# Scores and values of a two-layer attention kernel on 64x64 quadrants of the array, and VectorE's order around them

## The chip, the cores and the metric

The kernel runs on one core of one Trainium2 chip. The metric is the device time of one execution in microseconds (us), the median of several runs. Profiles are of one further execution. PE is TensorE (PEld its weight loads), DVE is VectorE, ACT is ScalarE, POOL is GpSimd and SP is SyncE.

## What is computed

Eight images x of 256 channels and 32 x 32 positions go through two layers; all numbers are fp32. S is 1024 positions, a head has 64 channels.

```python
# layer 0
qkv = (xt @ w_qkv + b_qkv).reshape(B, S, 8, 3 * 64)
q, k, v = split(qkv, 3, axis=-1)
attn = einsum('bihd,bjhd->bijh', q, k) * SCALE
attn = softmax(attn, axis=1)                 # over the queries i
res = einsum('bijh,bjhd->bihd', attn, v)
x = res @ w_out + b_out + xt
# layer 1
t = t + attention(layer_norm(t), W)          # one head of 256 channels
t = t + mixture_of_experts(layer_norm(t))    # 8 experts, the best 2 per token
```

In layer 0 the softmax runs over the queries, so that each key j has a maximum and a sum over all 1024 queries. The kernel therefore holds keys on the partitions and queries along the row: one row of scores has all that the softmax of a key needs, and the division by the sum can be put on the key's value vector instead of on the 1024 weights.

## The kernel before

One image after the other goes through layer 0 (`layer0`), layer 1's attention (`attend`) and the routing. The experts of the first seven images are computed together after layer 0 of the last image; the last image is done with all eight experts beside the collecting of the others' results.

`layer0` has 32 steps, (g, j): g is one of four pairs of heads, j one of eight blocks of 128 keys. A step makes the scores of both heads (`score`, L390): for head h and half n of the queries, one matmul of the head's 64 channels (partitions h * 64 and up) and 128 keys, into one bank of the score tile `psc`, which has two banks and comes from a pool of three. VectorE takes the negated maximum of the first half (`first_max`, L401) and then that of the second half together with the first (`soften`, L413). ScalarE takes the exponential of the whole tile with that maximum and sums it (L423). VectorE takes the reciprocal of both heads' sums (L430) and multiplies the step's values with it (L432, `vs`). Two steps later (LAG), `gather_values` multiplies `vs` with the exponentials and adds to `po` (L448): two banks, one for each half of the queries, head 0 on partitions 0 to 63 and head 1 on 64 to 127, accumulated over the eight blocks of keys. After the last block ScalarE copies both banks to `res` (L457), and the next pair of heads takes the same two banks.

The order on TensorE is written out in the loop at the end of `layer0`. In turn `at` it issues the first half of head 0 of this step, the second half of head 1 of the step before, the second half of head 0 and the first half of head 1 of this step, and then four matmuls of the values of step `at` - 2. In blocks 3 and 5 of the first three pairs it also projects queries or keys of the next pair (`project`, L299; VectorE takes them out of PSUM, L289). On VectorE the order is set in part by `issue_after`. From the second image on, the routing of the image before (`gates`, `dispatch`) is a generator that is taken one portion further in each turn: small VectorE operations first, then 16 portions of a cast (L764) and a scattering DMA that GpSimd issues (L766). In the last image the plan of the experts (`plan_blocks`) lies beside the last steps.

SyncE's queue holds transfers only. During layer 0 these are the load of the next image (`load_x`, L92) and the store of the sums of the image before (L1160), both issued ahead of the first values. For the first image it also fills the rows and packs the experts' weights (L245 to L277).

Of the kernel before, what the change touches and what calls it, by code (L numbers as in the profile page):

```python
# [10 lines left out]
F32 = mybir.dt.float32  # L11
I32 = mybir.dt.int32
AF = mybir.ActivationFunctionType
ALU = mybir.AluOpType
AX = mybir.AxisListType


@with_exitstack
def kernel(
# [23 lines left out]
    nc = tc.nc  # L43
    P = 128
# [3 lines left out]
    DK = 64  # L48
    SCALE = DK ** (-0.5)
    NCC = C // P  # L50
    NT = S // P
    NH2 = S // 512
# [316 lines left out]
    def layer0(b, xT, begun, routing):  # L369

        v, qks = begun.v, begun.qks
        array = None
        res = one.tile([P, NPAIR, S], F32, tag="res", name=f"res_{b}")
        steps = [(g, j) for g in range(NPAIR) for j in range(NT)]
        LAG = 2
        seconds = {}  # L380
        pss, firsts, nmaxes, exps, sums, vss = {}, {}, {}, {}, {}, {}
        po = None

        def score(at, h, n):
            g, j = steps[at]
            q, k = qks[g]
            if n == 0:
                pss[at, h] = big(f"psc_{b}_{g}_{j}_{h}")
            r = slice(h * DK, (h + 1) * DK)
            mm = nc.tensor.matmul(  # L390
                pss[at, h][:, ts(n, 512)], k[r, ts(j, P)], q[r, ts(n, 512)], start=True, stop=True
            )
            if n == 1:

                tc.declare_no_dep(mm.ins, firsts.pop((at, h)).ins, reason="the other bank")

        def first_max(at, h):

            g, j = steps[at]
            nmax = small.tile([P, 1], F32, tag="nmax1", name=f"nmax1_{b}_{g}_{j}_{h}")  # L400
            firsts[at, h] = nc.vector.tensor_reduce(  # L401
                nmax, pss[at, h][:, ts(0, 512)], AX.X, ALU.max, negate=True
            )
            nmaxes[at, h] = nmax

        def soften(at, h):

            g, j = steps[at]
            ps = pss.pop((at, h))
            if h == 0:  # L410
                sums[at] = small.tile([P, 2], F32, tag="sums", name=f"sums_{b}_{g}_{j}")
            nmax = small.tile([P, 1], F32, tag="nmax", name=f"nmax_{b}_{g}_{j}_{h}")
            seconds[h] = nc.vector.tensor_scalar(  # L413
                scrap,
                ps[:, ts(1, 512)],
                -1.0,
                nmaxes.pop((at, h)),
                ALU.mult,
                ALU.min,
                accum_out=nmax,  # L420
            )
            ex = expp.tile([P, 1024], F32, tag="exps", name=f"ex_{b}_{g}_{j}_{h}")
            nc.scalar.activation(  # L423
                ex, ps, AF.Exp, bias=nmax, scale=1.0, accum_out=sums[at][:, h : h + 1]
            )
            exps[at, h] = ex
            if h == 1:

                rs = small.tile([P, 2], F32, tag="rs", name=f"rs_{b}_{g}_{j}")
                nc.vector.reciprocal(rs, sums.pop(at))  # L430
                vs = four.tile([P, 2, DK], F32, tag="vs", name=f"vs_{b}_{g}_{j}")
                nc.vector.tensor_mul(  # L432
                    vs,
                    v[:, j, ts(g, P)].rearrange("p (h d) -> p h d", d=DK),
                    rs.unsqueeze(2).to_broadcast([P, 2, DK]),
                )
                vss[at] = vs

        def gather_values(at):
            nonlocal po  # L440
            g, j = steps[at]
            if j == 0:
                po = [acc(f"po_{b}_{g}_{n}") for n in range(NH2)]
            vs = vss.pop(at)
            exs = [exps.pop((at, h)) for h in range(2)]
            for n in range(NH2):
                for h in range(2):
                    mm = nc.tensor.matmul(  # L448
                        po[n][h * DK : (h + 1) * DK, :],
                        vs[:, h, :],  # L450
                        exs[h][:, ts(n, 512)],
                        start=(j == 0),
                        stop=(j == NT - 1),
                    )
            if j == NT - 1:
                for n in range(NH2):
                    nc.scalar.copy(res[:, g, ts(n, 512)], po[n])  # L457
            return mm

        last = len(steps) - 1  # L460
        for at in range(last + LAG + 1):
            if at <= last:
                score(at, 0, 0)
            if 0 < at <= last + 1:
                score(at - 1, 1, 1)
                soften(at - 1, 1)
            if at <= last:

                with tc.issue_after(seconds[1].ins) if 1 in seconds else nullcontext():
                    first_max(at, 0)  # L470
                score(at, 0, 1)
                score(at, 1, 0)
                soften(at, 0)
                with tc.issue_after(seconds[0].ins):
                    first_max(at, 1)
            if at == 0:
                begun.rest()
                next(routing, None)
            if at >= LAG:
                array = gather_values(at - LAG)  # L480
            if at <= last:
                g, j = steps[at]
                if g + 1 < NPAIR and j in (3, 5):
                    if j == 3:
                        qks.append([])
                    qks[g + 1].append(project(b, xT, g + 1, len(qks[g + 1])))
                if array is not None:
                    with tc.issue_after(firsts[at, 1].ins), tc.issue_after(array.ins):
                        next(routing, None)
        for _ in routing:  # L490
            pass


        t1 = one.tile([P, NT, C], F32, tag="t1", name=f"t1_{b}")
        n = 1024 // C
        for i in range(0, NT, n):
            pt = big(f"pt_x_{b}_{i}")
            for j in range(n):
                for cc in range(NCC):
                    nc.tensor.transpose(  # L500
                        pt[:, j * C + cc * P : j * C + (cc + 1) * P], xT[:, cc, ts(i + j, P)], ident
                    )
            nc.vector.tensor_add(
                t1[:, i : i + n, :],
                pt.rearrange("p (j c) -> p j c", c=C),
                b_o.unsqueeze(1).to_broadcast([P, n, C]),
            )
        for i in range(NT):
            pr = acc(f"pr_{b}_{i}")
            for g in range(NPAIR):  # L510
                nc.tensor.matmul(  # L511
                    pr[:, :C], res[:, g, ts(i, P)], wo[:, g, :], start=(g == 0), stop=(g == NPAIR - 1)
                )
            nc.vector.tensor_add(t1[:, i, :], pr[:, :C], t1[:, i, :])
        return t1
# [703 lines left out]
```

## Time and profile before

| | |
|---|---|
| median of 3 runs | 2549.14 us (2547.66 to 2549.50) |
| the profiled execution's own time | 2515.67 us |
| its span in the profile | 2513.9 us |
| mean granted clock of TensorE | 0.995 |
| TensorE busy | 2475.7 us, 98% |
| VectorE busy | 1547.4 us, 62% |
| ScalarE busy | 890.6 us, 35% |
| layer 0 of the second image: from 285.96 us to about 439 us | 153 us |

The profiled execution was shorter than the median of the runs by 33 us. A program matmul in fp32 shows as two matmul records and two weight loads. A line of the groups reads: line, engine, operation, out<-in, sizes, count, then busy time and the mean in ns of one, and the idle time ahead of it with what ended it. A line of the timeline reads: start, length, engine, line, operation, and in brackets the idle time before and what ended it.

### The profile page before, as it was taken

How to read it: one execution, taken by the hardware profiler on the slowest of the kernel's cores; microseconds unless marked ns; L12 is line 12 of the kernel's file. 1: busy time of each engine (PE TensorE's matmuls, PEld its weight loads, DVE VectorE, ACT ScalarE, POOL GpSimd, SP SyncE). 2: the span in 40 equal slices, each digit the busy share in tenths (PEclk: the TensorE clock that was granted, in tenths of full speed). 3: DMA queues.
4: the chain of work that ended last, by engine and by line, in shares of the span. 5: the costliest groups of instructions: out<-in, count | busy, mean ns of one | idle time of the engine just before them, and what ended most of it. 6: DMA issues, size and time to landing. Idle time of an engine off the chain costs nothing.

```text
span 2513.9 us, 27737 instructions
## 1 busy us (share of the span) xinstructions
PE 2475.7 (98%) x9919; PEld 1300.1 (52%) x9919; DVE 1547.4 (62%) x3836; ACT 890.6 (35%) x1491; POOL 385.7 (15%) x383
## 2 busy tenths in 40 slices
PE   9999999999999999999999999999999999999799
PEld 3346533653366335633563356434643388886476
DVE  5765677557755775577647764777467753334653
ACT  2551355124512452155314441354135512221222
POOL 0000002000200010001100010001000334444652
PEclk9999999999999999999999999999999999999899
DMA  7992000000000000000000010000000256664353
GB/s 284 385 360 69 34 3 32 17 17 0 28 24 17 1 24 28 9 9 18 34 1 17 13 38 1 17 11 24 1 17 7 74 171 220 213 212 141 125 174 115
DMA packets 82515, 187.62 MB, mean 75 GB/s; under 512 B 13992, under 2 KB 23880, under 8 KB 80584
## 3 DMA queue, kind: packets, MB, share of 16 engines
q1 hardware_dynamic: 57368, 118.65, 13.2%
q0 software_dynamic: 25008, 67.20, 8.5%
q8 instruction: 78, 1.28, 0.2%
q14 instruction: 61, 0.50, 0.1%
HBM read 100.49 MB, written 110.90 MB: 84 GB/s over the span
## 4 chain that ended last, share of the span: by engine, by line
PE 93%; DVE 3%; DMA 2%; ACT 1%; issue 1%; SPq 0%; ACTq 0%; POOL 0%; POOLq 0%; DVEq 0%
PE psc L390 20%; PE po L448 19%; PE pqk L299 9%; PE py L571 9%; PE ps L545 8%; PE pr L511 4%; PE pv L335 4%; PE ph L906 4%; PE pe L931 3%; PE pdy L1113 2%; PE px L530 2%; PE pa L564 2%; PE pdh L1089 2%; PE pt_n L232 1%; PE px L896 1%; DMA wb_x<-wpack,w_at 1%
## 5 line engine op out<-in xcount | busy, mean ns | idle before, releaser
L423 ACT ACTIVATE ex<-psc,nmax 128x1024 f32<-128x1024 f32 x512 | 570.6, 1114 | 556.8 <-DVE scrap L413 492.8
L390 PE MATMUL psc<-qk,qk 64*128 64x512 f32 x2048 | 549.4, 621 | 4.2 <-ACT ex L423 4.0
L448 PE MATMUL po<-ex,vs 128*64 128x512 f32 x2048 | 495.9, 605 | 0.0
L413 DVE TENSOR_SCALAR_CACHE_REDUCE scrap<-psc,nmax 128x512 f32<-128x512 f32 x512 | 384.2, 750 | 160.1 <-PE psc L390 128.0
L390 PEld LDWEIGHTS psc<-qk,qk 64*128 64x128 f32 x2048 | 208.6, 185 | 326.2 <-ACT ex L423 173.4
L401 DVE TENSOR_REDUCE nmax<-psc 128x1 f32<-128x512 f32 x512 | 347.2, 678 | 9.5 <-PE psc L390 9.5
L448 PEld LDWEIGHTS po<-ex,vs 128*64 128x64 f32 x2048 | 124.8, 136 | 335.4 <-issue 211.8
L766 POOL DMA_INDIRECT rows<-n,d_at x112 | 108.9, 972 | 946.5 <-DVE d_at L764 940.0
L571 PE MATMUL py<-n,aT 128*128 128x256 f32 x1024 | 239.9, 388 | 4.8 <-DVE aT L566 4.8
L545 PE MATMUL ps<-nT,xa 128*128 128x512 f32 x512 | 236.5, 592 | 0.0
L299 PE MATMUL pqk<-xT,wqkv 128*128 128x512 f32 x512 | 235.0, 602 | 0.0
L571 PEld LDWEIGHTS py<-n,aT 128*128 128x128 f32 x1024 | 192.8, 192 | 68.6 <-DVE aT L566 43.7
L556 ACT ACTIVATE ex<-ps,nmax 128x1024 f32<-128x1024 f32 x64 | 71.3, 1115 | 341.1 <-DVE nmax L553 334.4
L692 POOL TENSOR_TENSOR t<-t,n 128x2048 f32<-128x2048 f32 x8 | 36.2, 4531 | 905.7 <-issue 629.8
L576 DVE SCALAR_TENSOR_TENSOR t<-py,rs,t 128x256 f32<-128x256 f32 x64 | 31.0, 484 | 215.4 <-PE py L571 215.4
L299 PEld LDWEIGHTS pqk<-xT,wqkv 128*128 128x128 f32 x512 | 93.3, 190 | 132.5 <-issue 93.6
L289 DVE TENSOR_SCALAR qk<-pqk,b_qk 128x512 f32<-128x512 f32 x100 | 75.1, 751 | 110.3 <-PE pqk L299 110.3
L545 PEld LDWEIGHTS ps<-nT,xa 128*128 128x128 f32 x512 | 93.6, 190 | 79.9 <-issue 73.6
L978 POOL DMA_INDIRECT yk<-y,yat x112 | 112.7, 1006 | 92.8 <-DVE o L1010 43.6
L335 PE MATMUL pv<-wqkv,xT 128*128 128x512 f32 x256 | 119.6, 597 | 1.1 <-ACT wqkv L105 1.1
L553 DVE TENSOR_REDUCE nmax<-ps 128x1 f32<-128x1024 f32 x64 | 78.3, 1224 | 59.7 <-PE ps L545 59.7
L511 PE MATMUL pr<-wo,res 128*128 128x256 f32 x512 | 111.8, 379 | 0.0
(191 smaller groups left out, 2439.2 us busy)
## 6 DMA issues: line engine op xcount, KB each, us to landing
rows<-wb SPq DMA_DIRECT2D x7, 8192.0 KB, 51.3
y<-yb SPq DMA_DIRECT2D x63, 256.0 KB, 2.7
xT<-in_x_dram SPq DMA_DIRECT2D x7, 1024.0 KB, 4.9
sums<-t SPq DMA_DIRECT2D x7, 1024.0 KB, 4.4
o<-sums SPq DMA_DIRECT2D x7, 1024.0 KB, 7.7
out_dram<-oT SPq DMA_DIRECT2D x14, 512.0 KB, 5.8
wpack<-in_L_ffn_w_dram SPq DMA_DIRECT2D x4, 1024.0 KB
wb<-in_L_ffn_w_dram SPq DMA_DIRECT2D x16, 256.0 KB, 2.9
```

The lines of the kernel that those rows point to most:

```text
L299: mm = nc.tensor.matmul(pq[:, ts(n, 512)], wqkv[:, cc, t, ts(g, P)], xT[:, cc, ts(n, 512)], start=(cc == 0), stop=(cc == NCC - 1),)
L335: nc.tensor.matmul(pv, self.xT[:, cc, ts(i, P)], wqkv[:, cc, 2, :], start=(cc == 0), stop=(cc == NCC - 1),)
L390: mm = nc.tensor.matmul(pss[at, h][:, ts(n, 512)], k[r, ts(j, P)], q[r, ts(n, 512)], start=True, stop=True)
L401: firsts[at, h] = nc.vector.tensor_reduce(nmax, pss[at, h][:, ts(0, 512)], AX.X, ALU.max, negate=True)
L413: seconds[h] = nc.vector.tensor_scalar(scrap, ps[:, ts(1, 512)], -1.0, nmaxes.pop((at, h)), ALU.mult, ALU.min, accum_out=nmax,)
L423: nc.scalar.activation(ex, ps, AF.Exp, bias=nmax, scale=1.0, accum_out=sums[at][:, h : h + 1])
L448: mm = nc.tensor.matmul(po[n][h * DK : (h + 1) * DK, :], vs[:, h, :], exs[h][:, ts(n, 512)], start=(j == 0), stop=(j == NT - 1),)
L511: nc.tensor.matmul(pr[:, :C], res[:, g, ts(i, P)], wo[:, g, :], start=(g == 0), stop=(g == NPAIR - 1))
L545: nc.tensor.matmul(psc[:, ts(n, 512)], xa[:, ec, ts(i, P)], nT[:, ec, ts(n, 512)], start=(ec == 0), stop=(ec == NCC - 1),)
L571: nc.tensor.matmul(py[:, :D], aT[:, ts(m, P)], n1[:, m, :], start=(m == 0), stop=(m == NT - 1))
L766: nc.gpsimd.indirect_dma_start(out=view[:, :], out_offset=bass.IndirectOffsetOnAxis(ap=at, axis=0), in_=n2[:, i, :], in_offset=None,)
L978: nc.gpsimd.indirect_dma_start(out=yk[:, i, k, :], out_offset=None, in_=self.group.y[:, :], in_offset=bass.IndirectOffsetOnAxis(ap=ats[k][ ...
```

## The change

Scores: each matmul of 64 channels by 128 keys becomes two of 64 by 64, one for each half of the keys, which go to partitions 0 to 63 and 64 to 127 of the same bank.

Values: each matmul of 128 keys by 64 channels becomes two of 64 keys. They are issued in two turns. In a turn, keys 0 to 63 go to one bank of `po` and keys 64 to 127 to the other; in the second turn the banks change places. So each bank is added to by the lower and the upper keys one after the other. Between two turns that add to the same bank, an ordering is put in with an empty instruction (`relay.nop()`) that waits for the one turn's matmul and that the next turn's first matmul waits for. It is issued on GpSimd for the first image and on SyncE for the others. The first turn stands between the two pairs of score matmuls, the second after them.

VectorE: the reciprocal and `vs` move into a function `divide`. They stood, by `issue_after`, around the first maximum of the next step's head 1: the reciprocal ahead of it, `vs` behind. Now both stand behind the second maximum of the next step's head 0 and ahead of the first maximum of its head 1.

The number of instructions on VectorE and ScalarE stays as it is. The two copies out of `po` (L457) keep their place on ScalarE, behind the exponential of the same turn's head 0, with the second bank first.

```diff
+BEHIND = mybir.DependencyInfo(mybir.DependencyClass.Sync, mybir.DependencyReason.DATA)
...
-        seconds = {}
+        seconds, turned = {}, {}
+
+        relay = nc.gpsimd if b == 0 else nc.sync
...
-            mm = nc.tensor.matmul(
-                pss[at, h][:, ts(n, 512)], k[r, ts(j, P)], q[r, ts(n, 512)], start=True, stop=True
-            )
-            if n == 1:
-
-                tc.declare_no_dep(mm.ins, firsts.pop((at, h)).ins, reason="the other bank")
+            for c in range(2):
+                mm = nc.tensor.matmul(
+                    pss[at, h][ts(c, DK), ts(n, 512)],
+                    k[r, j * P + c * DK : j * P + (c + 1) * DK],
+                    q[r, ts(n, 512)],
+                    start=True,
+                    stop=True,
+                )
+                if n == 1:
+
+                    tc.declare_no_dep(mm.ins, firsts[at, h].ins, reason="the other bank")
...
+        def divide(at):
+
+            g, j = steps[at]
+            rs = small.tile([P, 2], F32, tag="rs", name=f"rs_{b}_{g}_{j}")
+            nc.vector.reciprocal(rs, sums.pop(at))
+            vs = four.tile([P, 2, DK], F32, tag="vs", name=f"vs_{b}_{g}_{j}")
+            divided = nc.vector.tensor_mul(
...
+        def gather_values(at, turn):
...
+            past = dict(turned)
+            for half in range(2):
+                keys = ts(half, DK)
+                n = (half + turn) % 2
                 for h in range(2):
                     mm = nc.tensor.matmul(
-                        po[n][h * DK : (h + 1) * DK, :],
-                        vs[:, h, :],
-                        exs[h][:, ts(n, 512)],
-                        start=(j == 0),
-                        stop=(j == NT - 1),
+                        po[n][ts(h, DK), :],
+                        vss[at][keys, h, :],
+                        exps[at, h][keys, ts(n, 512)],
+                        start=(j == 0 and turn == 0),
+                        stop=(j == NT - 1 and turn == 1),
                     )
+                    if h == 0 and (j > 0 or turn > 0):
+                        tc.add_manual_dep(mm.ins, past[1 - half].ins.name, BEHIND)
+
+                turned[half] = relay.nop()
+                tc.add_manual_dep(turned[half].ins, mm.ins.name, BEHIND)
...
                 score(at - 1, 1, 1)
                 soften(at - 1, 1)
+            if at >= LAG:
+                gather_values(at - LAG, 0)
...
                 with tc.issue_after(seconds[0].ins):
+                    ahead = divide(at - 1) if at > 0 else seconds[0]
+                with tc.issue_after(ahead.ins):
                     first_max(at, 1)
+            elif at == last + 1:
+                divide(last)
...
             if at >= LAG:
-                array = gather_values(at - LAG)
+                array = gather_values(at - LAG, 1)
```

More of the change, by code (lines that the diff above doesn't have):

```diff
@@ L426, in soften @@
             exps[at, h] = ex
[L427 to L437, printed above, removed]
@@ L439, in gather_values @@
-        def gather_values(at):
+        def divide(at):
[4 more added lines that the diff above has]
+            divided = nc.vector.tensor_mul(
+                vs,
+                v[:, j, ts(g, P)].rearrange("p (h d) -> p h d", d=DK),
+                rs.unsqueeze(2).to_broadcast([P, 2, DK]),
+            )
+            vss[at] = vs
+            return divided
@@ L440, in gather_values @@
+        def gather_values(at, turn):
             nonlocal po
             g, j = steps[at]
-            if j == 0:
+            if j == 0 and turn == 0:
                 po = [acc(f"po_{b}_{g}_{n}") for n in range(NH2)]
-            vs = vss.pop(at)
-            exs = [exps.pop((at, h)) for h in range(2)]
-            for n in range(NH2):
+            past = dict(turned)
+            for half in range(2):
+                keys = ts(half, DK)
+                n = (half + turn) % 2
                 for h in range(2):
@@ L455, in gather_values @@
+                        stop=(j == NT - 1 and turn == 1),
+                    )
+                    if h == 0 and (j > 0 or turn > 0):
+                        tc.add_manual_dep(mm.ins, past[1 - half].ins.name, BEHIND)
+                turned[half] = relay.nop()
+                tc.add_manual_dep(turned[half].ins, mm.ins.name, BEHIND)
+            if turn == 0:
+                return mm
+            vss.pop(at)
+            for h in range(2):
+                exps.pop((at, h))
             if j == NT - 1:
```

## The prediction

> **What bounds the kernel now.** I read the page first: TensorE is busy for 98% of the span and holds 93% of the chain that ended last; layer 0's scores (L390) and values (L448) have 39% of that chain between them. No other engine is near.
>
> ```profile
> PE 2475.7 (98%) x9919; PEld 1300.1 (52%) x9919; DVE 1547.4 (62%) x3836; ACT 890.6 (35%) x1491; POOL 385.7 (15%) x383
> ...
> L390 PE MATMUL psc<-qk,qk 64*128 64x512 f32 x2048 | 549.4, 621 | 4.2 <-ACT ex L423 4.0
> L448 PE MATMUL po<-ex,vs 128*64 128x512 f32 x2048 | 495.9, 605 | 0.0
> ```
>
> The shape before the operand says which part of the array an instruction uses: scores 64 rows x 128 columns, values 128 x 64. Each program matmul is two records (1024 in the program, 2048 here). Next the timeline, for what a record costs where nothing is switched, and for what runs side by side.
>
> ```profile
> 276.25 3.60 PE L299 MATMUL pqk<-xT,wqkv 128*128 128x512 f32 x8
> ...
> 279.69 1.88 PE L335 MATMUL pv<-wqkv,xT 128*128 128x512 f32 x4
> ...
> 284.96 1.07 PE L599 MATMUL pl<-n2T,rT 128*32 128x256 f32 x16
> ```
>
> Eight whole-array records take 279.69 - 276.25 = 3.44 us, 0.43 each: I call this a slot. The 16 records of pl (256 columns, four column strips) fill 1.07 us where one after the other would be 16 x 0.215 = 3.44, so four strips do run together. Then one step of layer 0:
>
> ```profile
> 402.69 2.04 PE L390 MATMUL psc<-qk,qk 64*128 64x512 f32 x8
> ...
> 403.87 0.75 DVE L413 TENSOR_SCALAR_CACHE_REDUCE scrap<-psc,nmax 128x512 f32<-128x512 f32 x1 [0.69 <-PE psc L390]
> ...
> 404.55 0.68 DVE L401 TENSOR_REDUCE nmax<-psc 128x1 f32<-128x512 f32 x1
> ...
> 404.66 1.94 PE L448 MATMUL po<-ex,vs 128*64 128x512 f32 x8
> ...
> 405.35 0.75 DVE L413 TENSOR_SCALAR_CACHE_REDUCE scrap<-psc,nmax 128x512 f32<-128x512 f32 x1
> ...
> 406.03 0.16 DVE L430 RECIPROCAL rs<-sums 128x2 f32<-128x2 f32 x1
> 406.11 0.67 DVE L401 TENSOR_REDUCE nmax<-psc 128x1 f32<-128x512 f32 x1
> 406.20 1.11 ACT L423 ACTIVATE ex<-psc,nmax 128x1024 f32<-128x1024 f32 x1 [0.27 <-DVE rs L430]
> ...
> 406.53 2.06 PE L390 MATMUL psc<-qk,qk 64*128 64x512 f32 x8
> 406.69 0.28 DVE L432 TENSOR_TENSOR vs<-v,rs 128x128 f32<-128x128 f32 x1
> 406.89 0.15 DVE L764 CAST d_at<-d_to 128x1 int32<-128x1 f32 x1
> ```
>
> Scores start at 402.69, values at 404.66, scores again at 406.53: a step is 3.84 (3.87 in the next). Its 16 records run in pairs, so 8 slots = 3.43. The other 0.41 is two changes between 64x128 and 128x64, 0.20 each. VectorE is free for about 0.67 a step, waiting for scores. Last, where one pair of heads ends (8 steps):
>
> ```profile
> 410.04 1.11 ACT L423 ACTIVATE ex<-psc,nmax 128x1024 f32<-128x1024 f32 x1 [0.28 <-DVE rs L430]
> ...
> 411.14 1.07 ACT L457 COPY res<-po 128x512 f32<-128x512 f32 x2
> ...
> 412.35 0.20 PEld L448 LDWEIGHTS po<-ex,vs 128*64 128x64 f32 x4 [0.76 <-ACT res L457]
> ```
>
> ScalarE copies the sums out of po behind an exponential, and the next values need them gone. Scores cover this just now: 410.38 to 412.35 is the usual 1.97.
>
> **What the skill says.** TensorEngine Tiling (Array Packing), Key Properties: a change of tiling mode, not of the tile, drains TensorE, and tiles work independently; the 0.20 per change agrees. Same page, Gotcha 1: different row tiles may not use one PSUM bank at the same time; that is why the change needs its relay, and the trace shows no such case. TensorE: Matmul & The Clock Gate, Measured speedup vs the span model: row and column tiles compose (16 tiles gave 10.6x). Pairs by row and strips by column are in this trace, quadrants are not.
>
> **The change, part by part.** Times are in us; a step begins with its first set of scores at 0.
>
> *Quadrants.* Scores and values become 2048 + 2048 instructions of 64x64, four at a time: a set is two slots, 0.86, and a step is scores, values, scores, values = 8 slots = 3.43, with no change of mode. Less is excluded, since each record still streams 512 columns; more is rival 3 or the 3.60 below. The 24 plain steps per image can save 0.41. The six with a projection (128x128) had three changes and keep two: 0.20 each. Issue is no limit by pl: 32 loads and matmuls went out in its 1.07, 0.033 each, where a slot of four quadrants has 0.43/8 = 0.054.
>
> *The relay.* A value set waits for the empty instruction on SyncE (GpSimd in image 0) that waits for the set before. Behind it on TensorE stand all later matmuls. Its cover is one score set: the earlier set's last record starts at 0.43 and is modelled at 0.59, so it ends at 1.02, and the next value set is due at 1.72: 0.70. No row has this trip. Bounds from hops: TensorE to VectorE 0.05, VectorE to GpSimd 0.27 (403.19 to 403.46), ScalarE to a weight load 0.15; so 0.2 to 0.5. I take 0.35: hidden, nothing. Were the scores gone (the image's last two steps), it costs about 0.5. On SyncE the queue ahead holds the image's load and the sums store, issued at 285.65 and 286.09, long before the first values at 297.54; GpSimd is empty in image 0 until its addition at 281.09.
>
> *VectorE's order.* vs now runs ahead of the second head's first maximum and needs the reciprocal. Start to start: second maximum 0.68, first maximum to the second that uses it 0.80, second maximum 0.68, reciprocal to vs 0.20 (0.16 and 0.04 for the dependence), vs 0.20, first maximum 0.80: 3.36, under 3.43. But the loop through everything is tight: third set at 1.72, VectorE 1.07 later (402.69 to 403.87, less 0.11 of mode change) at 2.79, then 0.68 + 0.20 + 0.20 + 0.80 to the next second maximum at 4.67, exponential 0.85 later (405.35 to 406.20), 1.11 long, 0.20 to the matmul (0.15 to its load, as above, and 0.05): 6.83, where the scores that take this buffer are due at 6.86. I take 3.46 per plain step; bounds 3.43 (all hidden) and 3.60 (reciprocal and vs as late as 0.14 more). Saving 24 x 0.39 + 6 x 0.20 = 10.6 per image, x8 = **-84.5**.
>
> *Head-pair ends.* The second maximum at 2.79 leads to the exponential at 3.64, the copies 1.10 later, 1.07 long, and 0.14 to TensorE: 5.95. The next values are now due after one score set only, at 3.43 + 0.86 = 4.29. Stall 1.66, three times per image: 24 x 1.66 = **+40**. Bounds 0 and 2.0 each.
>
> *Routing work.* For images 1 to 7 the previous image's routing runs on VectorE between a first and a second maximum. About 0.22 of it (one small operation or a cast) hides in the 0.80. Before, the idle 0.67 took the rest; now it is on the tight loop. Three operations add 0.5, four add 0.75. In steps beside a projection they hide (it gives 3.4). Left are steps 6, 7, 8 (0.5 each) and 14, 16 (0.75 each): 3.0, less 0.3 of slack: 2.7 x 7 = **+19**. Bounds 0 and 30. The plan for the experts puts some 7 on VectorE in image 7's last steps; about **+4** more than now is exposed.
>
> *Ends of an image.* The first values fit into a wait for exponentials (-0.4), the last two steps wait for the relay (+0.6): **+1** in all.
>
> **Sum.** -84.5 + 40 + 19 + 4 + 1 = -20. The profiled span is 2513.9, its own time 2515.7: 2495. The median of the runs is 2549.1, 33 above that execution, and I carry the difference over: **2529**.
>
> **Rivals.**
> 1. TensorE alone decides (0.25): exponentials, copies and routing find cover, as they do now, and 84 is gained: 2465; with half of the stalls, 2495. For it: nothing but TensorE waits today. Against: the copies' chain has no slack even now.
> 2. The relay is late (0.18), the case that ends slower. Place: each of 60 value sets per image, 480 in all. It decides from 0.70, and 20/480 = 0.04 beyond eats the gain. At 0.85: 480 x 0.15 = +72: 2601. For it: three engines' queues lie in it, and no row shows the way back from SyncE. Against: each hop that is seen is at most 0.27.
> 3. Quadrants don't run four wide, so that the change doesn't do what it says (0.05): a set takes four slots, a step 6.9; far above 3000. Against: rows and columns each overlap here.
>
> **How the numbers follow.** My case has 0.52, with a range of its own from 2505 to 2550. The range that should hold 8 in 10 is 2466 to 2580: it leaves out rival 3, over half of rival 2 and a little of rival 1, and takes in plain steps of 3.60 (27 more) and the stalls' upper bounds in part. A measurement tells about 0.2% (5 us) from no change. Faster: 0.25 + 0.44 of mine = 0.69. Same: 0.06. Slower: 0.17 of rival 2, 0.05 and 0.03 = 0.25.
>
> **What would show it.** Right: rows with 64*64 at 4096 records each, score and value sets 0.86 apart, plain steps near 3.45, TensorE's wait for the copies up from 18 us to some 55, VectorE's idle for scores nearly gone. Value loads that wait for SyncE in plain steps would be rival 2; sets of 1.7 rival 3; head-pair ends without a stall, or routing steps as short as plain ones, rival 1.

## The result, and the profile after

| | before | after |
|---|---|---|
| median of 4 runs each | 2549.32 us | 2526.41 us (2521.92 to 2530.92) |
| ratio, with its 95% interval | | 0.9908 (0.9883 to 0.9932) |
| the profiled execution's own time | 2515.67 us | 2521.92 us |
| layer 0, sum over the eight images | 1225.2 us | 1197.2 us |
| from layer 0's end to the next layer 0 | 107.51 us | 108.05 us |
| from layer 0's end in the last image to the program's end | 509.4 us | 539.4 us |

The change made the kernel faster by 22.9 us; 20 had been forecast. The two profiled executions can't be set against each other as wholes. What follows layer 0 of the last image, which the change does not touch, depends on the job, that is, on which runs were made together. It took 531 to 540 us in every profile of a later job in which the kernel before ran at 2544 us, and 509 to 512 in every profile of three jobs in which it ran at 2516 to 2518, old and new kernels alike. Of the two profiles here, the one of before has the short stage and the one of after the long one. So I compare stages. "Layer 0" is from an image's first score record to the start of its last value record. There the change gains 27.9 us, and 7 x 0.54 = 3.8 are given back behind it: 24.1, which agrees with the medians.

First the page of the changed kernel: busy time by engine, then the rows of the scores and the values.

```profile
PE 2421.3 (96%) x14015; PEld 1334.8 (53%) x14015; DVE 1565.1 (62%) x3836; ACT 887.7 (35%) x1491; POOL 386.4 (15%) x383
...
L463 PE MATMUL po<-ex,vs 64*64 64x512 f32 x4096 | 612.8, 593 | 25.4 <-ACT res L482 21.3
L395 PE MATMUL psc<-qk,qk 64*64 64x512 f32 x4096 | 613.4, 596 | 17.3 <-ACT ex L432 16.3
```

There are twice as many records, of 64x64, and each is about as long as one of 64x128 was (596 ns against 621). The busy times of these two rows don't tell how wide they run, since the rows overlap; the timeline below does: a set of eight records is followed by the next set after 0.86. That is two slots of 0.43, so four records run at a time. (Eight of 64x128 held TensorE for 1.97, 402.69 to 404.66 in the timeline of before: four slots and a change of mode.) New is the idle time ahead of the values: 21.3 us that ended with ScalarE's copies. It had been 0.0 on that row.

Next the timeline of the changed kernel, image 0: the last plain step of a pair of heads, and the pair's end.

```profile
67.63 1.04 PE L395 MATMUL psc<-qk,qk 64*64 64x512 f32 x8
...
68.49 1.04 PE L463 MATMUL po<-ex,vs 64*64 64x512 f32 x8
...
69.35 1.04 PE L395 MATMUL psc<-qk,qk 64*64 64x512 f32 x8
...
69.78 0.15 PEld L463 LDWEIGHTS po<-ex,vs 64*64 64x64 f32 x4 [0.28 <-POOLq L473]
70.20 1.04 PE L463 MATMUL po<-ex,vs 64*64 64x512 f32 x8
...
71.06 1.04 PE L395 MATMUL psc<-qk,qk 64*64 64x512 f32 x8
...
71.27 1.11 ACT L432 ACTIVATE ex<-psc,nmax 128x1024 f32<-128x1024 f32 x1 [0.34 <-DVE rs L441]
...
72.38 1.06 ACT L482 COPY res<-po 128x512 f32<-128x512 f32 x2
...
73.01 0.20 PEld L463 LDWEIGHTS po<-ex,vs 64*64 64x64 f32 x4 [1.79 <-ACT res L482]
73.01 1.13 PE L463 MATMUL po<-ex,vs 64*64 64x512 f32 x6 [0.91 <-ACT res L482]
...
73.49 0.14 PEld L463 LDWEIGHTS po<-ex,vs 64*64 64x64 f32 x2 [0.29 <-ACT res L482]
...
73.92 0.60 PE L395 MATMUL psc<-qk,qk 64*64 64x512 f32 x2
...
73.97 0.59 PE L463 MATMUL po<-ex,vs 64*64 64x512 f32 x2
```

A set starts every 0.86, and a step is 71.06 - 67.63 = 3.43. The value load at 69.78 waited for the empty instruction (here on GpSimd), but 0.42 ahead of its matmul at 70.20, which is on time. At the pair's end the values were due at 71.92; the copies, which stand behind the exponential of 71.27, let the first half go at 73.01 and the second at 73.49. From then on score and value records stand between one another in groups of two. I read this as the upper and the lower 64 rows of the array, the two row groups, running out of phase until the next projection brings them together; the trace doesn't name a record's rows.

The lengths of all steps say the same at a glance (worked out from the trace; a step is sixteen score records, counted from the image's first):

```
after, image 0   5.98 2.74 3.85 7.27 3.43 7.23 3.43 3.43 3.43 3.43 4.63 7.64 3.43 7.23 3.43 3.43 3.43 3.43 4.63 7.64 3.43 7.23 3.43 3.43 3.43 3.43 4.63 3.67 3.43 3.43 3.43
after, image 3   6.19 2.80 3.85 7.27 3.43 7.23 3.43 3.84 3.80 3.95 4.59 8.09 3.73 7.42 3.43 4.09 3.43 4.09 4.59 7.64 3.43 7.23 3.43 3.43 3.43 3.43 4.63 3.67 3.43 3.43 3.44
after, image 1   6.19 2.80 3.83 7.72 8.84 7.69 3.43 3.84 3.80 3.95 4.59 8.09 3.73 7.49 3.43 4.09 3.43 4.09 4.59 7.64 3.43 7.23 3.43 3.43 3.43 3.43 4.63 3.67 3.43 3.43 3.43
```

A step with a projection is 7.23, and a pair's end costs 4.63 - 3.43 = 1.20 and 7.64 - 7.23 = 0.41 in the next step: 1.61. (Behind the third end, which no projection follows, the second part is 0.24 in the next step, and the rest at the image's end.) Image 3 has the routing of the image before on VectorE: single steps of 3.8 to 4.1. Image 1 has one thing more, near its first projection (7.72, 8.84 and 7.69 for 7.27, 3.43 and 7.23). In the timeline of that place:

```profile
299.97 2.42 PE L395 MATMUL psc<-qk,qk 64*64 64x512 f32 x8
...
302.29 2.66 PE L463 MATMUL po<-ex,vs 64*64 64x512 f32 x14
...
303.81 1.11 ACT L432 ACTIVATE ex<-psc,nmax 128x1024 f32<-128x1024 f32 x1 [7.53 <-PE po L463]
...
305.59 2.63 PE L463 MATMUL po<-ex,vs 64*64 64x512 f32 x13
```

Fourteen and thirteen value records in a row: the program's order on TensorE is another one here. All values of two steps stand bunched behind the projection, and ScalarE is without work for 7.53 us.

Layer 0 by image, for the kernels of this study (us):

| kernel | image 0 | image 1 | images 2 to 6, usual | image 7 | sum |
|---|---|---|---|---|---|
| before | 151.7 | 152.7 | 152.75 | 156.2 | 1225.2 |
| after | 145.0 | 154.9 | 148.6 | 154.2 | 1197.2 |
| no_copies | 140.2 | 150.4 | 144.0 | 148.3 | 1159.3 |
| old_tiles_no_copies | 151.9 | 152.7 | 152.7 | 156.2 | 1225.2 |
| old_tiles_new_order | 151.7 | 152.9 | 152.9 | 156.0 | 1226.1 |
| quadrants_old_order | 160.8 | 171.6 | 164.7 | 168.5 | 1325.3 |
| quadrants_old_pinned | 148.8 | 156.2 | 150.5 | 154.5 | 1212.2 |
| relay_pool_1 | 145.0 | 154.3 | 148.6 | 154.4 | 1196.8 |
| relay_pool_all | 145.0 | 154.3 | 154.2 | 163.9 | 1234.3 |
| routing_split | 145.0 | 147.9 | 147.4 | 151.6 | 1181.4 |
| split_late | 143.6 | 146.5 | 146.0 | 151.6 | 1171.4 |
| split_project | 141.8 | 144.7 | 144.65 | 150.3 | 1160.0 |
| split_copies_first | 142.5 | 144.7 | 144.5 | 148.7 | 1158.3 |
| all_mended | 141.0 | 143.8 | 143.8 | 148.0 | 1151.7 |

### The profile page after: what moved, and what is told of

It reads as the page before. It is cut to its first block, busy times and chain, and to the rows that moved or that the text cites. A ratio compares the mean times of both kernels' runs of the same rounds, so it can differ in the third digit from the quotient of the medians.

```text
span 2520.2 us, 37152 instructions
## 1 busy us (share of the span) xinstructions
PE 2421.3 (96%) x14015; PEld 1334.8 (53%) x14015; DVE 1565.1 (62%) x3836; ACT 887.7 (35%) x1491; POOL 386.4 (15%) x383
## 4 chain that ended last, share of the span: by engine, by line
PE 72%; DVE 9%; ACT 3%; issue 2%; DMA 1%; another core or an unknown queue 1%; ACTq 0%; DVEq 0%; SPq 0%; POOLq 0%
PE po L463 13%; PE psc L395 12%; PE pqk L300 8%; PE py L602 7%; PE ps L576 6%; PE pr L542 4%; PE ph L937 4%; PE pe L962 3%; PE pv L336 3%; DVE scrap L422 3%; PE pdy L1144 2%; PE pdh L1120 2%; PE px L561 2%; PE pa L595 2%; ACT ex L432 2%
## 5 line engine op out<-in xcount | busy, mean ns | idle before, releaser
L463 PE MATMUL po<-ex,vs 64*64 64x512 f32 x4096 | 612.8, 593 | 25.4 <-ACT res L482 21.3
L395 PE MATMUL psc<-qk,qk 64*64 64x512 f32 x4096 | 613.4, 596 | 17.3 <-ACT ex L432 16.3
L422 DVE TENSOR_SCALAR_CACHE_REDUCE scrap<-psc,nmax 128x512 f32<-128x512 f32 x512 | 383.9, 750 | 118.3 <-PE psc L395 98.7
L395 PEld LDWEIGHTS psc<-qk,qk 64*64 64x64 f32 x4096 | 188.0, 132 | 320.7 <-issue 167.8
L463 PEld LDWEIGHTS po<-ex,vs 64*64 64x64 f32 x4096 | 187.2, 132 | 285.0 <-issue 91.3
```

The lines of the kernel that those rows point to most:

```text
L395: mm = nc.tensor.matmul(pss[at, h][ts(c, DK), ts(n, 512)], k[r, j * P + c * DK : j * P + (c + 1) * DK], q[r, ts(n, 512)], start=True, stop ...
L422: seconds[h] = nc.vector.tensor_scalar(scrap, ps[:, ts(1, 512)], -1.0, nmaxes.pop((at, h)), ALU.mult, ALU.min, accum_out=nmax,)
L463: mm = nc.tensor.matmul(po[n][ts(h, DK), :], vss[at][keys, h, :], exps[at, h][keys, ts(n, 512)], start=(j == 0 and turn == 0), stop=(j == ...
```

## The experiments

My theory after the result: TensorE's slots are the gain, and four losses stand against it, the copies at the pairs' ends, the routing on VectorE, the order in image 1, and the relay at an image's end. The rivals stand in the expectations. The kernels ran in four jobs. The kernel before took 2544.0 us in the one with no_copies, old_tiles_new_order, quadrants_old_order and relay_pool_1, 2517.6 in the one with old_tiles_no_copies, quadrants_old_pinned, relay_pool_all and routing_split, 2516.8 in the one with the three ways to mend the pairs' ends, and 2516.2 in that of all_mended. A kernel is compared with the runs of before in its own job; where a distance to the changed kernel or between two jobs is given, it is the difference of two such comparisons. The totals in the expectations are on the level of the first two numbers of this document's result; what counts of them is the distance to before or to the changed kernel.

**The pairs' ends.** Both kernels without the copies' wait; the copies read the transposed image, so layer 0's sums are left out:

```diff
-                    nc.scalar.copy(res[:, g, ts(n, 512)], po[n])
+                    nc.scalar.copy(res[:, g, ts(n, 512)], xT[:, n, 0:512])
```

> The changed kernel with ScalarE's copies at the end of a head pair reading the transposed image instead of po, so that nothing waits for po to be emptied; the layer's sums are left out of the output. Theory: the copies are what a pair's end loses, 1.61 us in each of 24 places: layer 0 of images 2 to 6 goes from 148.6 to about 143.8, the whole from 2526 to about 2487. Rival: behind the copies stands the next wait (the exponentials that VectorE's chain makes late), and less than 0.5 of the 1.61 goes: 2515 or more.

Measured 2487.1 us, 0.978 of before (0.9765 to 0.9795). The theory holds: the steps of 4.63 become 3.43, those of 7.64 become 7.22, layer 0 is shorter by 4.8 in image 0 and by 4.6 in images 1 to 6, 38.0 in all. By the medians it is 34 below the changed kernel: 0.43 comes back behind each layer 0 (108.48 for 108.05). No other wait of like size stood behind the copies.

> The kernel before with the copies reading the transposed image instead of po; the layer's sums are left out. Theory: in the old order scores cover the copies just to the end, so there is nothing to gain: layer 0 of the images stays at 152.7 within 0.6, the whole within 5 us of the kernel before. Rival: the copies cost the kernel before as much as the changed one (1.55 per place): layer 0 at 148, the whole 37 shorter.

Measured 2519.6 us, 1.0015 (1.0008 to 1.0021), with layer 0 at 152.74 as before (the 2 us lie behind it: 107.93 instead of 107.51). In the old order the copies cost nothing; the whole 38 is a price of the new one.

**VectorE's order.** First the new order on the old tiles (the reciprocal and `vs` stand in `divide`, as in the change):

```diff
                 with tc.issue_after(seconds[0].ins):
+                    ahead = divide(at - 1) if at > 0 else seconds[0]
+                with tc.issue_after(ahead.ins):
                     first_max(at, 1)
```

> The kernel before with VectorE's new order alone. Theory: VectorE waits 0.67 us for scores in each step, which takes the 0.3 by which the first maximum of head 1 moves: no change, within 5 us of the kernel before. Rival: the routing's steps have no room left for it and become longer by 0.2 to 0.3: +5 to +15.

Measured 2545.5 us, 1.0003 (0.9994 to 1.0011); layer 0 152.9 against 152.75. It does nothing by itself.

Then the quadrants without it:

```diff
+            if h == 1:
+                divide(at)
...
                 with tc.issue_after(seconds[0].ins):
-                    ahead = divide(at - 1) if at > 0 else seconds[0]
-                with tc.issue_after(ahead.ins):
                     first_max(at, 1)
-            elif at == last + 1:
-                divide(last)
```

> The quadrants and the relay, with VectorE's old order: the reciprocal ahead of the first maximum of head 1, the scaled values behind it. Theory: scaled values then come 0.49 later; from a step's first value set to the next: 0.86 to the third score set, 1.07 to its second maximum, 0.68 to the reciprocal, 0.08 and 0.60 to the scaled values, 0.28 and 0.05 to TensorE: 3.62 instead of 3.43, so 0.19 in some 26 steps of 8 images, +40, of which some 15 come back because the loop through everything gets 0.4 of room and hides the routing: +15 to +40, so 2541 to 2566. Rival: the scaled values are not on the path, and the shorter loop gains: 2526 or less, by up to 15.

Measured 2647.8 us, 1.0408 (1.0394 to 1.0423), far outside both. The timeline of this kernel shows where its plain steps lose:

```profile
429.15 1.11 ACT L432 ACTIVATE ex<-psc,nmax 128x1024 f32<-128x1024 f32 x1 [0.28 <-DVE scrap L422]
...
430.39 0.17 DVE L443 RECIPROCAL rs<-sums 128x2 f32<-128x2 f32 x1 [0.73 <-ACT ex L432]
...
430.59 0.29 DVE L445 TENSOR_TENSOR vs<-v,rs 128x128 f32<-128x128 f32 x1
430.80 0.74 DVE L422 TENSOR_SCALAR_CACHE_REDUCE scrap<-psc,nmax 128x512 f32<-128x512 f32 x1
```

This is not the old order. Left free, the scheduler put the reciprocal ahead of head 0's second maximum, where VectorE stands 0.73 us for the exponential of 429.15, and the second maximum, whose scores had ended by 430.0, stands behind it. A step is 3.97. In the kernel before, too, the code ties only the maxima with `issue_after`; the places of the reciprocal and of `vs`, which the description of the change puts down to it, were the scheduler's choice.

The step is not the whole of it. A pair's end takes 5.4 to 8.5 in this kernel, and near many of the ends the granted clock of TensorE falls to half: 17 times in layer 0, 65 us together, which may cost up to 32 of the 128 us that layer 0 is longer than in the changed kernel (an estimate: half of 65). Records that begin in such a stretch are longer, here in image 0:

```profile
116.91 1.07 PE L395 MATMUL psc<-qk,qk 64*64 64x512 f32 x2
...
120.30 0.60 PE L395 MATMUL psc<-qk,qk 64*64 64x512 f32 x2
```

So the run answers another question than the one I asked. I repeated it with the old order written out (`invert` is the reciprocal; `divide` is left with `vs`):

```diff
                 with tc.issue_after(seconds[0].ins):
-                    ahead = divide(at - 1) if at > 0 else seconds[0]
+                    ahead, rs = invert(at - 1) if at > 0 else (seconds[0], None)
                 with tc.issue_after(ahead.ins):
                     first_max(at, 1)
+                if at > 0:
+                    with tc.issue_after(firsts[at, 1].ins):
+                        divide(at - 1, rs)
```

> Quadrants and relay with VectorE's old order, now pinned: second maximum of head 0, reciprocal, first maximum of head 1, scaled values. Theory: the scaled values come 0.49 later and the loop from a value set over them to the next value set is 3.62 instead of 3.43: 0.19 in each plain step, layer 0 of images 2 to 6 from 148.6 to 151 to 154, the whole 15 to 40 above the changed kernel. Rival: the scaled values have room, and the shorter chain on VectorE hides the routing: layer 0 of images 2 to 6 at 146 to 148.6, the whole up to 15 below the changed kernel.

Measured 2509.5 us, 0.9966 of before in its job (0.9954 to 0.9977), that is 8 below before where the changed kernel is 23 below. The timeline:

```profile
400.78 1.04 PE L395 MATMUL psc<-qk,qk 64*64 64x512 f32 x8
...
401.48 0.28 DVE L447 TENSOR_TENSOR vs<-v,rs 128x128 f32<-128x128 f32 x1
...
401.81 0.21 PEld L467 LDWEIGHTS po<-ex,vs 64*64 64x64 f32 x8 [0.88 <-DVE vs L447]
...
404.44 1.04 PE L395 MATMUL psc<-qk,qk 64*64 64x512 f32 x8
```

The values, due at 401.64, wait for vs, and a plain step is 3.66 (3.62 expected). Image 0 loses 3.73 by it, while the routing's cost falls from 3.55 to 1.76 per image (images 2 to 6 less image 0), since VectorE's loop has room: 15 us net, the lower end of what was expected (images 2 to 6 at 150.5, just under the 151 to 154 of the expectation). The new order on VectorE is worth 15 us, and only beside the quadrants' order of sets.

**The relay's place.**

```diff
-        relay = nc.gpsimd if b == 0 else nc.sync
+        relay = nc.gpsimd if b <= 1 else nc.sync
```

> The empty instruction of the second image is put on GpSimd too, as in the first. Theory: the second image loses 6.4 us on the images after it because its order on TensorE is another one (all values of two steps in one bunch behind the first projection), and with GpSimd it gets the regular order: its layer 0 goes from 154.9 to about 148.6, the whole from 2526 to about 2520. Rival: the loss belongs to the second image itself (its routing is the first one, its loads are late), and it keeps 154 to 155: no change, within 2 us.

Measured 2520.6 us, 0.9909 (0.9894 to 0.9924), with layer 0 of image 1 at 154.3: by the number, the rival. But the steps show that two things moved. The first projection is at 7.27 and 3.43 as in the other images, so the bunch and its 6.3 are gone; and from step 19 on, while GpSimd scatters, most steps are 0.57 longer, 5.7 in all. If that is the relay's doing, it must return in every image once all relays are there:

```diff
-        relay = nc.gpsimd if b == 0 else nc.sync
+        relay = nc.gpsimd
```

> The empty instruction on GpSimd in all images. Theory: the order of the second image is mended (6.3), but while GpSimd issues the scatters (0.97 us each, one per step) the empty instruction stands behind them and comes 0.57 late in every step, as in the second image of the kernel with GpSimd there, which lost 5.7: seven images lose 5.7 each, 40, less 6.3: layer 0 of images 2 to 6 at 154.3, the whole 34 above the changed kernel, at 2560. Rival: the scatters were late in the second image alone (its values still come from the first plan): images 2 to 6 stay at 148.6, the whole at 2520.

Measured 2529.3 us, 1.0053 (1.0036 to 1.0069), 11.7 above before where the changed kernel is 22.9 below: 34.6 above it (34 expected), images 2 to 6 at 154.2. This is my second rival, a late relay, made real. How it comes about differs from what I wrote. In the timeline of image 2:

```profile
657.68 1.07 PE L395 MATMUL psc<-qk,qk 64*64 64x512 f32 x8
...
658.73 0.14 DVE L795 CAST d_at<-d_to 128x1 int32<-128x1 f32 x1
...
659.05 0.24 PEld L463 LDWEIGHTS po<-ex,vs 64*64 64x64 f32 x8 [1.19 <-DVE d_at L795]
659.08 1.09 PE L463 MATMUL po<-ex,vs 64*64 64x512 f32 x8 [0.34 <-POOLq L473]
659.15 0.97 POOL L797 DMA_INDIRECT rows<-n,d_at  x1 [3.03 <-DVE d_at L795]
```

The values were due at 658.54 and start at 659.08, ahead of the scatter's 0.97 us. They wait for the cast: in GpSimd's queue the empty instruction stands behind the scatter, and the scatter waits for the cast of 658.73. The trace has the turn's second empty instruction at 658.92, 0.04 after the cast's end and 1.01 after the first.

**The routing on VectorE.** The relay stays on GpSimd only for image 0 and the first pair of image 1, ahead of the scatters; the routing's operations are dealt out in smaller shares.

```diff
+            relay = nc.gpsimd if b == 0 or (b == 1 and g == 0) else nc.sync
...
             nc.vector.tensor_mul(hot, hot, rank)
             nc.vector.tensor_reduce(best, hot, AX.X, ALU.max)
+            yield
...
         nc.vector.tensor_scalar_max(total, total, 1e-12)
+        yield
         nc.vector.reciprocal(total, total)
...
                     in_offset=None,
                 )
-                yield
+                if i % 2:
+                    yield
```

(Three more `yield` of the same kind stand in the other shares.)

> The empty instruction on GpSimd in the first image and in the first pair of heads of the second, and the routing's small operations in shares of one or two instead of three to five, with two casts and scatters to a step instead of one. Theory: the routing costs what lies over about 0.22 us in a step, so shares of two (about 0.4) cost little: of the 2.5 in each of seven images some 1.2 goes, 8 in all, and 6.3 goes in the second image: layer 0 of images 2 to 6 at 147.4, of image 1 at the same, the whole 14 below the changed kernel, 2512. Rival: VectorE's loop has no room at all, and every operation costs its length wherever it stands: images 2 to 6 stay at 148.6, only the 6.3 goes, 2520.

Measured 2476.8 us, 0.9839 (0.9823 to 0.9856), 40.8 below before and so 17.9 below the changed kernel. Images 2 to 6 at 147.4, image 1 at 147.9: both terms as expected. So what the routing costs is what lies over the cover in each step, not its sum.

**Three ways to mend the pairs' ends,** all on top of the split routing. The first gives TensorE a projection to do while the copies run:

```diff
-                if g + 1 < NPAIR and j in (3, 5):
-                    if j == 3:
+                first = 1 if g else 3
+                if g + 1 < NPAIR and j in (first, 5):
+                    if j == first:
```

> The kernel with the split routing, and in it the first projection for the third and the fourth pair of heads moved from block 3 to block 1, where it stands on TensorE right behind the last values of the pair before. Theory: the copies out of po are late by 1.61 us at a pair's end because TensorE has nothing else to do; a projection of 3.4 us lies over the chain to the copies (5.95 less 3.43), so two of three places per image lose nothing: layer 0 of images 2 to 6 from 147.4 to 144.2, the whole 26 below the split kernel. Rival: VectorE's and ScalarE's loop is what is late at a pair's end, and the projection with its two evictions of 0.75 only takes cover from block 3: 147 or more.

Measured 2456.2 us, 0.9762 (0.9745 to 0.9778): 60.6 below before, 19.8 below the split kernel. In the timeline the copies lie under the projection, and the values after it are on time:

```profile
70.94 3.70 PE L300 MATMUL pqk<-xT,wqkv 128*128 128x512 f32 x8
...
72.15 1.06 ACT L483 COPY res<-po 128x512 f32<-128x512 f32 x2
...
74.58 1.09 PE L395 MATMUL psc<-qk,qk 64*64 64x512 f32 x8
...
75.48 1.04 PE L464 MATMUL po<-ex,vs 64*64 64x512 f32 x8
```

Image 0, which has no routing, gains 3.22 = 2 x 1.61. Images 2 to 6 gain 2.75: some of the routing had hidden beside the projection of block 3, and where that stood, step 19 takes 3.89 now, for 3.43 in image 0.

The second puts the copies ahead of the exponential (`ends` marks the turn with a pair's last values, `emptied` holds its two copies):

```diff
+                if ends:
+                    array = gather_values(at - LAG, 1)
                 soften(at, 0)
...
+            free = h == 0 and ends
+            with tc.issue_after(emptied.pop().ins) if free else nullcontext(), (
+                tc.issue_after(emptied.pop().ins) if free else nullcontext()
+            ):
```

> The split kernel with the two copies put ahead of the exponential of the same turn on ScalarE. Theory: the copies can start when the last values end, at 3.6 in the step, and take 1.07; the exponential starts at 4.66 instead of 3.64, and the loop of 6.83 against 6.86 has no room for it: a place loses 1.0 instead of 1.61, three per image: layer 0 of images 2 to 6 from 147.4 to 145.6, the whole 15 shorter. Rival: both waits count, the copies' and the late exponential's, and it stays at 147 to 149.

Measured 2455.0 us, 0.976 (0.9743 to 0.9776), 61.8 below before: 2.9 per image where 1.8 was expected. The pair's end has a step of 3.78 instead of 4.63. Its timeline:

```profile
71.08 1.07 ACT L487 COPY res<-po 128x512 f32<-128x512 f32 x2 [0.35 <-PE po L468]
...
71.72 1.13 PE L468 MATMUL po<-ex,vs 64*64 64x512 f32 x6
72.03 1.13 ACT L436 ACTIVATE ex<-psc,nmax 128x1024 f32<-128x1024 f32 x1
...
72.20 0.14 PEld L468 LDWEIGHTS po<-ex,vs 64*64 64x64 f32 x2 [0.29 <-ACT res L487]
...
73.13 1.12 ACT L436 ACTIVATE ex<-psc,nmax 128x1024 f32<-128x1024 f32 x1
73.30 0.19 PEld L395 LDWEIGHTS psc<-qk,qk 64*64 64x64 f32 x4 [0.54 <-ACT ex L436]
```

I had put the loop without room on the wrong exponential. The loop of 6.83 against 6.86 runs through head 1's. The copies hold up head 0's (72.03), which frees the score buffer that head 1 of the next step takes, and this one has 0.2 of room (3.64 + 1.11 + 0.20 = 4.95 in the prediction's terms, against 3.43 + 1.72 = 5.15). What is left of the pair's end shows on TensorE. The values of the second bank begin at 72.20, 0.48 after those of the first, behind the second copy. Then head 1's scores, due at 72.58 (the step began at 70.86), load their weights at 73.30, when head 0's exponential is over: 0.72 late. A pair's end still costs 3.78 - 3.43 and 7.64 - 7.23, 0.76 together.

The third lets the first values of a pair start later:

```diff
+            late = at >= LAG + NT and (at - LAG) % NT == 0
-            if at >= LAG:
+            if at >= LAG and not late:
                 gather_values(at - LAG, 0)
...
+            if late:
+                gather_values(at - LAG, 0)
```

> The split kernel with the first turn of a pair's first block put behind the step's scores, next to its second turn. Theory: the first values are due at 5.15 instead of 4.29, so the copies are 0.80 late, and the second turn waits 0.35 for the empty instruction, which no scores cover here: 1.15 instead of 1.61, three places: layer 0 of images 2 to 6 from 147.4 to 146.0, the whole 11 shorter. Rival: VectorE gets its scores earlier and the wait is the copies' alone, so all of 0.86 is gained: 144.8.

Measured 2467.6 us, 0.981 (0.9793 to 0.9827), 49.2 below before, images 2 to 6 at 145.96, where 146.0 was expected; the whole is 8 below the split kernel, for 11. It is the weakest of the three.

The first and the second concern different places, since no projection is left for the third pair's end:

> The split kernel with the projections in block 1 (which cover two of a layer's three pair ends), and at the third end, which no projection follows, the copies ahead of the exponential. Theory: the two add up, since they concern different places: of the third end's 1.2 over a plain step 0.85 goes, as in the kernel with the copies first (4.63 to 3.78): layer 0 of images 2 to 6 from 144.65 to 143.8, the whole 67 below the kernel before on the same chip, 7 below the one with the projections alone. Rival: the third end's gain in that kernel came from the steps ahead of it (a phase that the projection has changed), and it stays at 144.6, 60 below the kernel before.

The edit is that of split_project, with that of split_copies_first for `at - LAG == (NPAIR - 1) * NT - 1` alone. Measured 2449.08 us, 0.9733 of before (0.972 to 0.9746): 67.1 below before, layer 0 of images 2 to 6 at 143.8. On the page of this kernel the wait for the copies is gone from the values' row:

```profile
L395 PE MATMUL psc<-qk,qk 64*64 64x512 f32 x4096 | 579.7, 596 | 12.8 <-ACT ex L436 12.7
L468 PE MATMUL po<-ex,vs 64*64 64x512 f32 x4096 | 571.9, 591 | 4.1 <-DVE vs L447 3.4
```

## Why the prediction was right, step by step

| step | predicted | measured | from |
|---|---|---|---|
| quadrants, with VectorE's order | -84.5 | -92 | image 0 of no_copies less before, 140.20 - 151.66 = -11.46, x8 |
| pairs' ends | +40 | +38 | after less no_copies |
| routing | +19 | +17 | images 2 to 6 less image 0: 3.55 after, 1.09 before; x7 |
| the plan in image 7 | +4 | +2 | image 7 less images 2 to 6: 5.6 after, 3.5 before; 1.5 of it by the clock |
| ends of an image | +1 | +4 | 0.54 behind each layer but the last |
| image 1's order | not seen | +6 | 154.94 less 148.57 |
| sum | -20 | -25 | stages together: -24; medians: -23 |

That the total came within 3 us is in part luck: the quadrants gained 7 more than predicted and three losses were 6 smaller, while the image's end and image 1's order, 9 together, were not foreseen. The 33 us between the profile of before and its runs were carried over without a reason; they held, and the stage behind the last layer 0, 30 longer in the profile of after, is where they fit.

*Quadrants.* Right, and the plain step was a little better than taken: 3.43, my lower bound, instead of 3.46 (24 x 8 x 0.03 = 6 of the difference). The loop of 6.83 against 6.86 through VectorE and ScalarE does fit. It was no idle worry: the operations put on it showed in the steps with routing. (The step after the one that the prediction shows is 3.85, 410.38 - 406.53, not 3.87; the sum rests on 3.85.)

*The relay.* Hidden, as predicted. Its trip is shorter than the 0.35 that I took: in one place of image 1 the trace has a value set's end near 400.87 (the ends of matmuls are modelled), 0.04 to 0.1 later SyncE's event, and at 401.02 the arrival on TensorE, so 0.15, half a microsecond ahead of the matmul. In the list of waits, value loads that wait for SyncE stand 128 times:

```profile
DVE scrap L422 <- PE psc L395: 98.7, 247, 1.3
...
PEld po L463 <- ACT res L482: 49.4, 48, 1.8
...
PEld po L463 <- SPq L473: 42.9, 128, 1.0
...
PE po L463 <- ACT res L482: 21.3, 24, 0.9
```

That is idle time of the loads, which run ahead of the matmuls; the matmuls' own row has no wait for SyncE that large. The same list shows the copies: 49.4 us at the loads, where I said some 55.

*Pairs' ends.* Right in mechanism and size: 38.0 over 24 places is 1.58 for 1.66 (1.61 in image 0, some 1.5 in images 1 to 6). The loss takes two forms, 1.20 of plain waiting and 0.41 by the row groups out of phase, which I had not foreseen; the split is read off the steps, and no kernel separates the two.

*Routing.* Right: 2.46 per image for 2.7. It stands in steps 7 to 9 (0.4 to 0.5 each), 15 and 17 (0.66 each), close to where I placed it; steps 11 and 12 are longer than in image 0 by 0.45 and 0.30, but they were by 0.40 and 0.47 in the kernel before. VectorE's wait for scores did not nearly vanish, though (98.7 us after, 128.0 before): in image 0 it is 1.3 at each pair's end, 0.6 beside each projection and 0.2 in a plain step.

*The plan in image 7.* Of the +2, some 1.5 are not VectorE's work. From 1944.4 the trace has the granted clock at half for 3.41 us, and a set of scores there is nearly twice as long as one of 1.04:

```profile
1944.70 1.99 PE L395 MATMUL psc<-qk,qk 64*64 64x512 f32 x8 [2.35 <-ACT ex L432]
1946.46 1.71 PE L463 MATMUL po<-ex,vs 64*64 64x512 f32 x8
1948.00 1.03 PE L395 MATMUL psc<-qk,qk 64*64 64x512 f32 x8
```

The two sets take 3.30, 1944.70 to 1948.00, where no_copies takes 1.76 for the same two (1912.37 to 1914.13) at the full clock, after the same wait of 2.35: 1.54 longer. What sets the half clock off was not tried.

*What failed.* "Nothing" for the relay on SyncE in image 1: I read the queue for what would delay the empty instruction while the kernel runs, and did not compare the order on TensorE image by image, though that can be read ahead of a run. There the scheduler had bunched the values. That the bunch is the cost is shown (relay_pool_1, routing_split). Why the scheduler did it in this image alone is open. One difference is SyncE's queue: in image 1 the store of the sums and the load of the next image are issued at 280.03 and 280.46, as layer 0 begins, and in image 2 the store alone (543.09), the load 106 us ahead of it; that this is the cause was not tried. The image's end failed too. The prediction's +1 was for the first values and the last two steps inside layer 0; the measured 0.54 lies behind the last value, where nothing was predicted. It is read off the stages and was not tried by itself.

*The rivals.* The first (all finds cover) falls with no_copies: 38 us had no cover. The second decides where the relay shares a queue with something that waits, as on GpSimd: +34.6. The third was never near.

## What to carry to other kernels

When a change takes a stage's slack away, list what that slack was hiding: here copies, small operations and an ordering, which with the image's end gave back 67 us of a gain of 92. Two thirds of that (45 us of layer 0) were won again by moving other work over them or by dealing them out. An empty instruction as a relay cost little here, but it takes on every wait that stands ahead of it in its engine's queue. An order that matters has to be written out; a scheduler that is left to choose can put a waiting instruction ahead of one that is ready.

## What had not been expected of the hardware

- Two row groups of the array can run out of phase: after one waits longer for its bank (73.01 and 73.49 in the timeline above), score and value records of 64x64 alternate in pairs. Plain steps behind a third end are 3.43 all the same; behind the first two, 0.41 shows in the step in which 128x128 instructions join them.
- The trip from TensorE over an empty instruction on SyncE and back took about 0.15 us in the place that was read.
- The granted clock of TensorE fell to half inside layer 0, for 3.41 or 6.83 us at a time, 17 times in quadrants_old_order and once in the changed kernel, never in the kernel before; records of 64x64 took 1.07 there for 0.59.
- The stage behind layer 0 of the last image, the same in all kernels, took 531 to 540 us in all profiles of one job and in that of the changed kernel, and 509 to 512 in that of before and in all profiles of the three other jobs, with a mean granted clock of 0.95 to 0.96 and of 0.97 to 0.98. What makes a job long is open.
